# Attention front brought beside the shared projection, and six preparation operations moved from VectorE to GpSimd

## The chip, the cores and the metric

The kernel runs on one core of a Trainium2 chip. The metric is the device time of one execution in microseconds (us), lower is better; a profiled execution adds a trace of every instruction. The engines are called PE (TensorE; PEld is its weight load), DVE (VectorE), ACT (ScalarE), POOL (GpSimd) and SP (SyncE, which only issues DMAs here). Each engine works through its own queue in order.

## The reference

An input x of 4 batches, 512 tokens and 1024 features goes through four layers, each in float32. Cut to what matters:

```python
x = x + L0_attn(layernorm(x))       # attention across the batch axis
x = x + L0_ffn(layernorm(x))        # linear + top-2 of 8 LoRA experts
x = x + L1_attn(layernorm(x))       # the part that the change touches
x = x + L1_ffn(layernorm(x))        # linear + a routed mixture of LoRAs
# L1_attn:
q   = rmsnorm(x @ wq_a.T) @ wq_b.T          # 32 heads of 64 + 64 (rope)
kv  = rmsnorm((x @ wkv_a.T)[..., :64]) @ wkv_b.T
q_pe, k_pe = rope(q_pe), rope(k_pe)
p   = softmax(causal(q_full @ k_full.T * scale))
out = (p @ v) @ wo.T
```

The residual and norm lines are abridged. Per head, `wq_b` and the key part of `wkv_b` are folded into one weight, so that the scores are taken directly against the 64 normalised latent values and the 64 rotated ones; the value part of `wkv_b` is folded into the output weight.

## The kernel before, in words

A float32 product is made of three matmuls with operands split into a high and a low part (`matmul3`, L140 to L145: high by low, low by high, high by high). So each operand needs a rounding copy (the high part, mostly ACT) and a subtraction (the low part, DVE or POOL).

The stages, by the time of the profile: 0 to 76 us the batch attention, to 330 the first feed-forward layer, 330 to 425 the shared projection, 425 to about 1500 the heads, to 1580 a passage, and to the end the second feed-forward layer.

**The shared projection** (L708 to L806) goes over 16 token tiles of 128 in steps s = 0 to 16. Step s makes the product `pq` of tile s (24 matmuls of 128x384), turns tile s+2 (`turn1`: 8 transposes, with copies by ACT and DVE to `hTh`, `hTl`) and finishes tile s−1 (`keep`, L758 to L781: transposes `pn`, results `qT`, `kT` written to DRAM, per batch in `q_d`, `kT_d`, `kF_d`, `k_d`). `kf` (L744 to L755) is the key of one tile. At steps 6 and 10 weights of queries are asked for (`fetch_query`), at 8 and 12 prepared (`prepare_query`, L641 to L655, with `wql` on POOL). When the four tiles of batch 0 are done, that batch is loaded back into slot A (`load_batch`, L660: 1 MB of queries, 0.5 MB of keys); batch 1 is loaded into slot B by the heads' loop at unit 2, and every later one six units ahead.

**The heads** (loop L1171 to L1210) are 128 units u = (g, b, i): 4 groups of heads, 4 batches, 8 heads i of the group. One unit is

- `query(u)` (L678): six 128x512 matmuls of the head's weight with the batch's latent queries; `rotate_query(u)` (L690): `qf` copied by ACT (L693), two products `t` by DVE from PSUM (L695, L696), then POOL's product and sum (L697, L698); `split_query(u)` (L701): `qh` by DVE (L705) and `ql` by POOL (L706);
- `scores(u)` (L861 to L893): four query tiles, 512, 384, 256 and 128 keys wide; each is masked and copied out of PSUM by a DVE operation that also takes the row's extremum `mn` (L882), then ACT takes the exponential with `mn` as bias and adds up the row (L885). For every second unit `divisors` (L841 to L856) inverts the sums of two units on DVE, writes them to DRAM (`r_d`) and reads them back spread over partitions (`rb`), all through SP;
- `turn(u−1)` (L897): ten transposes into `pst`, three copies to `pT`, two on ACT and one on DVE;
- `context(u−3)` (L911) for every second unit: the product of values and `pT` of two units in the bank `psv`, multiplied by `rb` on DVE (L925).

**Between these** the loop advances a filler by a number of steps that `per` (L1178) gives for three places of an iteration. The filler is the output product of the batch before (`project`, L971), spread over the eight heads; in batch 0 of groups 1 to 3 it takes the first four heads, and the last four have `prepare_output` (L1015 to L1137), which makes the output weights of the group: `block` (two matmuls into the bank `poa` or `pob`), `kept` (ACT's copy to a room in SBUF), `high` (ACT), `low` and `less` (DVE, L1051 and L1055). In group 0 the preparation starts with batch 0's first head, with (0, 1, 2). Output weights come to slot C by DMA.

**What sets the order.** The program is emitted in the order of these loops, and a scheduler fixes each engine's queue from it. `tc.issue_after(ins)` holds an instruction back until behind `ins` in the order; `low` and `less` are held behind the last mask (`turn_of`), and the table load of the exponential (L804) behind the projection's last scaling (`scaled`). PSUM has eight banks: in the projection two `pt`, one `pw` (named `po`), two `pn`, three `pq`; in the heads two `pss`, two `pst`, one each of `psq`, `psv`, `poa`, `pob`.

Of the kernel before, what the change touches and what calls it, by code (L numbers as in the profile page):

```python
# [9 lines left out]
F32 = mybir.dt.float32  # L10
FR = mybir.dt.float32r
AF = mybir.ActivationFunctionType
ALU = mybir.AluOpType
# [4 lines left out]
P = 128  # L18
# [28 lines left out]
def block_kernel(ctx: ExitStack, tc: tile.TileContext, a: dict, out: bass.AP):  # L47
# [43 lines left out]
    def f32(t):  # L91
        return t.bitcast(F32)
# [564 lines left out]
    def slot(k):  # L657
        return slots[k].tile([P, ND * W1B], F32, name="slot" + "ABC"[k])
# [42 lines left out]
    def split_query(u):  # L701
# [4 lines left out]
        G.tensor_tensor(l, f[:, P:S], f32(h), ALU.subtract)  # L706
        queries[u] = f, h, l

    wqs, batches = {}, {}
    with tc.tile_pool(name="c1_w", bufs=1, side="right") as wap, \  # L710
            tc.tile_pool(name="c1_work", bufs=2) as wk, \
            tc.tile_pool(name="c1_pt", bufs=2, space=PSUM) as ptp, \
            tc.tile_pool(name="c1_pw", bufs=1, space=PSUM) as pwp, \
            tc.tile_pool(name="c1_pn", bufs=2, space=PSUM) as pnp, \
            tc.tile_pool(name="c1_pq", bufs=3, space=PSUM) as pqp:
        for ch in range(1, ND):
            split_shared(wap, ch)

# [61 lines left out]
                nc.sync.dma_start(out=kF_d[b], in_=kF)  # L780

        hts, qk, scaled = hts1, {}, [None]
        stats1[TPB - 1] = statistics([x[:, t, :] for t in order[-NB:]], "c", 4)
        for s in range(NT + 1):
            if s < NT:
                qk[s] = project(s, hts[s])
            if s + 2 < NT:
                hts[s + 2] = turn1(s + 2, ptp)
            if s > 0:
                keep(s - 1, qk[s - 1])  # L790
                if order1[s - 1] == TPB - 1:
                    batches[0, 0] = load_batch(0, 0)
            if s in (6, 10):
                wq_raw = fetch_query(s // 4 - 1)
            if s in (8, 12):
                wqs[s // 4 - 2] = prepare_query(wq_raw, pwp)
            if s in (NT - 2, NT - 1):
                query(s - NT + 2, pwp, "po")
                rotate_query(s - NT + 2)
            if s == NT - 1:  # L800
                split_query(0)

                with tc.issue_after(scaled[0].ins):
                    A.activation(first, first, AF.Exp)  # L804
# [5 lines left out]
    with ExitStack() as c2:  # L810
# [13 lines left out]
        pss = heads.enter_context(tc.tile_pool(name="c2_pss", bufs=2, space=PSUM))  # L824
        pst = heads.enter_context(tc.tile_pool(name="c2_pst", bufs=2, space=PSUM))
        psv = heads.enter_context(tc.tile_pool(name="c2_psv", bufs=1, space=PSUM))

        OF = {3: 0, 2: 512, 1: 896, 0: 1152}


        scored = [None]
        sums_of = [None]

        turn_of = [None]

        turned_in = [rdp.tile([P, 32], F32, name=f"ri{k}") for k in range(2)]
        for t in turned_in:
# [22 lines left out]

        def scores(u):  # L861

            g, b, i_ = units[u]
            f, h, l = queries.pop(u)
            _, kT, kF, _ = batches[g, b]
            p = pp.tile([P, 1280], F32, name="p")
            mn = small.tile([P, TPB], F32, name="mn")
            if i_ % 2 == 0:
                sums_of[0] = small.tile([P, 2, TPB], F32, name="rs2")
            rs2 = sums_of[0]  # L870
            rs = rs2[:, i_ % 2, :]
            for i in range(TPB - 1, -1, -1):
                n = (i + 1) * P
                ps = pss.tile([P, S], F32, name="pss")
                if i == 0:
                    scored[0] = T.matmul(ps[:, 0:n], lhsT=f[:, 0:P], rhs=kF, start=True, stop=True)
                else:
                    at = slice((i - 1) * P, i * P)
                    matmul3(ps[:, 0:n], h[:, at], l[:, at], kT[:, 0, 0:n], kT[:, 1, 0:n],
                            start=True, stop=True)  # L880
                to = p[:, OF[i] : OF[i] + n]
                turn_of[0] = V.tensor_tensor_reduce(out=to, in0=ps[:, 0:n], in1=causal[:, S - n : S], scale=1.0,  # L882
                                                    scalar=-NEG, op0=ALU.add, op1=ALU.min,
                                                    accum_out=mn[:, i : i + 1])
                A.activation(to, to, AF.Exp, bias=mn[:, i : i + 1], scale=-1.0,  # L885
                             accum_out=rs[:, i : i + 1])
                if i > 0:
                    yield
            if i_ % 2:
                divisors(u, rs2)  # L890
            probs[u] = p
            yield


# [2 lines left out]
        def turn(u):  # L897

            p = probs.pop(u)
            pTs[u] = pT = tp.tile([P, 1280], F32, name="pT")  # L900
            for copy, js in ((A.copy, (0,)), (A.copy, (3, 1)), (V.tensor_copy, (2,))):
                ps = pst.tile([P, S], F32, name="pst")
                w = 0
                for j in js:
                    for i in range(j, TPB):
                        T.transpose(ps[:, w : w + P], p[:, OF[i] + j * P : OF[i] + (j + 1) * P], ident)  # L906
                        w += P
                copy(pT[:, AT[js[0]] : AT[js[0]] + w], ps[:, 0:w])  # L908
                yield
# [105 lines left out]
        def prepare_output(g, fetched):  # L1015

            wouts[g] = {}  # L1020
            room = raw()[:, 0 : 6 * 512].rearrange("p (k n) -> p k n", k=6)
            prs = [c + k for c in range(HG // 4) for k in (0, HG // 4)]
# [24 lines left out]

            def low(kind, at):
                h, l = wouts[g][kind][-1]
                with tc.issue_after(turn_of[0].ins):  # L1050
                    V.tensor_tensor(l, src(at), f32(h), ALU.subtract)  # L1051

            def less(to, a0, a1):
                with tc.issue_after(turn_of[0].ins):
                    V.tensor_tensor(src(to), src(a0), src(a1), ALU.subtract)  # L1055

            def steps():
                block(0, 0, "a")
                yield
                kept(0, "a")  # L1060
                high("b11", "a")
                block(0, 1, "b")
                yield
                low("b11", "a")
                kept(1, "b")
                yield
                less("b", "b", 0)
                block(1, 0, "a")
                yield
                high("t1", "b")  # L1070
                kept(0, "b")
                kept(2, "a")
                high("b21", "a")
                yield
                low("t1", "b")
                low("b21", "a")
                block(1, 1, "b")
                yield
                high("b22", "b")
                kept(3, "b")  # L1080
                yield
                low("b22", "b")
                less("b", "b", 0)
                block(2, 0, "a")
                yield
                high("t2", "b")
                kept(5, "a")
                less(3, 3, 1)
                yield
                low("t2", "b")  # L1090
                less("b", 2, "b")
                high("b11", "a")
                yield
                high("t4", "b")
                high("t3", 3)
                low("b11", "a")
                yield
                low("t4", "b")
                low("t3", 3)
                block(2, 1, "a")  # L1100
                yield
                kept(1, "a")
                yield
                less("a", "a", 5)
                block(3, 0, "b")
                yield
                high("t1", "a")
                kept(5, "a")
                kept(2, "b")
                high("b21", "b")  # L1110
                yield
                low("t1", "a")
                low("b21", "b")
                block(3, 1, "a")
                yield
                high("b22", "a")
                kept(3, "a")
                yield
                low("b22", "a")
                less("a", "a", 5)  # L1120
                yield
                high("t2", "a")
                less(3, 3, 1)
                yield
                low("t2", "a")
                less("a", 2, "a")
                high("t3", 3)
                yield
                high("t4", "a")
                low("t3", 3)  # L1130
                yield
                low("t4", "a")
                yield
# [37 lines left out]
        for u in range(NU + 3):  # L1171
# [3 lines left out]
            g, b = divmod(B, NB)  # L1175
            if i == 0 and B > 0:
                filler = project(*divmod(B - 1, NB))
            per = ((4, 1, 0) if i % 2 else (1, 1, 0)) if b else (2, 2, 2) if i >= HG // 2 else (3, 3, 1)  # L1178
            if B == 0:
                per = (0, 1, 2)  # L1180
            if b == 0 and i == (HG // 2 if g else 0) and g < NG:
# [6 lines left out]
            advance(sc)  # L1188
            advance(cx)
            advance(filler, per[0])  # L1190
            if u + 1 < NU:
                split_query(u + 1)
            advance(sc)
            advance(sc)
# [3 lines left out]
            if u < NU:  # L1198
# [2 lines left out]
                    wqs[2 * g + 2] = prepare_query(wq_raw, pso, "pob")  # L1201
                if (b, i) == (0, 0) and g > 0:
                    wqs[2 * g + 1] = prepare_query(wq_raw, pso, "pob")
            if u + 2 < NU:
                query(u + 2, psq, "psq")
            if u + 2 < NU:
                rotate_query(u + 2)
            advance(filler, per[2])
            advance(tn)
# [471 lines left out]
```

## Time and profile before

| what | value |
|---|---|
| median of three runs | 1758.72 us (1757.91 to 1758.85) |
| the profiled execution | 1762.22 us, its span 1760.4 us |
| busy PE, PEld | 1714.4 us, 1433.1 us |
| busy DVE, ACT, POOL | 1311.9 us, 901.5 us, 895.7 us |
| granted clock of TensorE, mean | 0.998 of full speed |
| DMA | 228.16 MB, mean 130 GB/s |

The span runs from the first to the last recorded instruction; the rest of the profiled time lies outside it. A window row gives the length, the busy time of PE, PEld, DVE, ACT and POOL with their instruction counts, the granted clock, the share of DMA time and GB/s. A timeline row gives start, duration, engine, line, operation, output and input; in brackets stands the idle time of the engine just before it and what ended it.

### The profile page before, as it was taken

The numbers are of one execution on the slowest core, as the hardware profiler recorded it, in microseconds if no ns is written. First come the engines' busy times: TensorE is split into PE (matmuls) and PEld (weight loads), VectorE is DVE, ScalarE is ACT, GpSimd is POOL, SyncE is SP. The second block draws the span as 40 slices with busy tenths as digits, with TensorE's granted clock in tenths as the row PEclk, the third lists the DMA queues.
The fourth block names the chain that finished last, engine by engine and source line by source line (L and its number), as shares of the span: only waits on it lengthen the run. The fifth ranks groups of instructions, "written<-read, shape, count | busy, mean of one in ns | idle before, by whom it ended". The sixth has DMA issues, their size and how long they took to land.

```text
span 1760.4 us, 31605 instructions
## 1 busy us (share of the span) xinstructions
PE 1714.4 (97%) x10536; PEld 1433.1 (81%) x10536; DVE 1311.9 (75%) x3517; ACT 901.5 (51%) x2316; POOL 895.7 (51%) x902
## 2 busy tenths in 40 slices
PE   6999999999999999999999999999999999989999
PEld 6999999998677777767777767777766777789998
DVE  6977885676887777787777687777778777687675
ACT  7422331365765555575555575555466555453332
POOL 0553541203566665556566546666545665675454
PEclk9999999999999999999999999999999999999999
DMA  4313543245324234353333352343353333843431
GB/s 192 135 40 115 184 162 108 90 137 162 108 97 143 80 119 137 120 163 111 107 117 117 111 191 94 99 143 94 130 177 123 120 103 113 322 182 124 136 117 61
DMA packets 131939, 228.16 MB, mean 130 GB/s; under 512 B 22272, under 2 KB 58752, under 8 KB 128448
## 3 DMA queue, kind: packets, MB, share of 16 engines
q1 hardware_dynamic: 131776, 226.13, 39.0%
q8 instruction: 84, 1.38, 0.3%
q14 instruction: 79, 0.65, 0.1%
HBM read 156.60 MB, written 71.83 MB: 130 GB/s over the span
## 4 chain that ended last, share of the span: by engine, by line
PE 87%; DVE 6%; DMA 3%; ACT 2%; POOL 1%; issue 1%; SPq 0%; DVEq 0%; ACTq 0%; POOLq 0%
PE psv L922 9%; PE pst L906 7%; PE po L143 4%; PE po L145 4%; PE po L144 4%; PE pss L143 4%; PE pss L144 4%; PE pss L145 4%; PE poa L143 3%; PE pob L143 3%; PE psq L143 3%; PE psq L145 3%; PE psq L144 3%; PE poa L145 3%; PE poa L144 3%; PE pob L145 3%
## 5 line engine op out<-in xcount | busy, mean ns | idle before, releaser
L885 ACT ACTIVATE p<-p,mn 128x512 f32<-128x512 f32 (+3 forms) x512 | 284.4, 559 | 208.0 <-DVE mn L882 207.7
L697 POOL TENSOR_TENSOR qf<-qf,ropeT 64x512 f32<-64x512 f32 x128 | 165.5, 1293 | 274.6 <-ACT qf L693 270.5
L882 DVE CUSTOM_DVE_ANT_0 p<-pss,causal 128x512 f32<-128x512 f32 (+3 forms) x512 | 231.5, 486 | 28.4 <-PE pss L145 23.2
L698 POOL TENSOR_TENSOR qf<-qf,t 64x512 f32<-64x512 f32 x128 | 166.2, 1299 | 43.3 <-DVE t L696 35.8
L906 PE MATMUL pst<-ident,p 128*128 128x128 f32 x1280 | 186.5, 274 | 0.7 <-ACT pT L908 0.7
L906 PEld LDWEIGHTS pst<-ident,p 128*128 128x128 f32 x1280 | 153.8, 141 | 26.0 <-ACT pT L908 2.7
L908 ACT COPY pT<-pst 128x512 f32<-128x512 f32 x256 | 141.7, 580 | 44.8 <-PE pst L906 43.7
L706 POOL TENSOR_TENSOR ql<-qf,qh 128x384 fp32r<-128x384 f32 x128 | 129.9, 1015 | 62.1 <-DVE qh L705 62.1
L143 PE MATMUL pss<-kT,ql 128*128 128x512 f32 (+2 forms) x384 | 144.6, 376 | 4.0 <-POOL ql L706 1.5
L957 POOL TENSOR_TENSOR cxl<-s,cxh 128x256 fp32r<-128x256 f32 x128 | 97.4, 768 | 88.5 <-ACT cxh L956 60.7
L143 PE MATMUL po<-w_h,hTl 128*128 128x384 f32 (+1 forms) x384 | 133.1, 347 | 1.1 <-DVE x L398 1.1
L144 PE MATMUL pss<-kT,qh 128*128 128x512 f32 (+2 forms) x384 | 130.9, 341 | 0.0
L145 PE MATMUL pss<-kT,qh 128*128 128x512 f32 (+2 forms) x384 | 130.3, 339 | 0.0
L145 PE MATMUL po<-w_h,hTh 128*128 128x384 f32 (+1 forms) x384 | 130.1, 339 | 0.0
L144 PE MATMUL po<-w_l,hTh 128*128 128x384 f32 (+1 forms) x384 | 129.7, 338 | 0.0
L908 DVE COPY pT<-pst 128x256 f32<-128x256 f32 x128 | 54.1, 423 | 94.1 <-PE pst L906 93.3
L693 ACT COPY qf<-psq 128x512 f32<-128x512 f32 x126 | 73.8, 586 | 67.7 <-PE psq L145 67.1
L695 DVE TENSOR_TENSOR t<-psq,ropeT 32x512 f32<-32x512 f32 x126 | 87.7, 696 | 23.4 <-ACT qf L693 19.4
L143 PEld LDWEIGHTS pss<-kT,ql 128*128 128x128 f32 x384 | 72.7, 189 | 35.4 <-POOL ql L706 11.4
L885 ACT ACTIVATION_READ_ACCUMULATOR p<-p,mn 128x1 f32 x512 | 97.3, 190 | 0.0
L696 DVE TENSOR_TENSOR t<-psq,ropeT 32x512 f32<-32x512 f32 x126 | 87.1, 691 | 1.8
L999 DVE TENSOR_TENSOR xs<-xs,pob 128x512 f32<-128x512 f32 x105 | 71.2, 678 | 19.4 <-PE pob L145 19.2
(564 smaller groups left out, 4961.1 us busy)
## 6 DMA issues: line engine op xcount, KB each, us to landing
xs<-x_d SPq DMA_DIRECT2D x128, 256.0 KB
x_d<-xs SPq DMA_DIRECT2D x128, 256.0 KB
slotC<-in_woT_dram SPq DMA_DIRECT2D x32, 512.0 KB
rb<-r_d SPq DMA_DIRECT2D x128, 128.0 KB
w_t<-raw SPq DMA_DIRECT2D x32, 288.0 KB
x<-in_x_dram SPq DMA_DIRECT2D x16, 512.0 KB
x_d<-x SPq DMA_DIRECT2D x32, 256.0 KB
slotA<-q_d SPq DMA_DIRECT2D x8, 1024.0 KB
```

What stands on the lines that cost most here:

```text
L143: T.matmul(ps, lhsT=al, rhs=bh, start=start, stop=False, **kw)
L144: T.matmul(ps, lhsT=ah, rhs=bl, start=False, stop=False, **kw)
L145: T.matmul(ps, lhsT=ah, rhs=bh, start=False, stop=stop, **kw)
L697: G.tensor_tensor(f[mid], f[mid], ropeT[mid, 0, :], ALU.mult)
L698: G.tensor_tensor(f[mid], f[mid], t2[mid], ALU.add)
L706: G.tensor_tensor(l, f[:, P:S], f32(h), ALU.subtract)
L882: turn_of[0] = V.tensor_tensor_reduce(out=to, in0=ps[:, 0:n], in1=causal[:, S - n : S], scale=1.0, scalar=-NEG, op0=ALU.add, op1=ALU.min, ...
L885: A.activation(to, to, AF.Exp, bias=mn[:, i : i + 1], scale=-1.0, accum_out=rs[:, i : i + 1])
L906: T.transpose(ps[:, w : w + P], p[:, OF[i] + j * P : OF[i] + (j + 1) * P], ident)
L908: copy(pT[:, AT[js[0]] : AT[js[0]] + w], ps[:, 0:w])
L922: T.matmul(ps[n * KVR : (n + 1) * KVR, S - w : S], lhsT=k[:, j, :], rhs=pTs[u + n][:, AT[j] : AT[j] + w], start=(j == 0), stop=(j == TPB - 1))
L957: G.tensor_tensor(l, src, f32(h), ALU.subtract)
```

## The change: what it does

1. The queries of units 0 to 3 are made in steps 9, 10, 13 and 15 of the shared projection (before: units 0 and 1 in steps 14 and 15, 2 and 3 in the heads' loop). Units 0, 1 and 2 are split one step after.
2. The masked scores of units 0 and 1 (`AHEAD = 2`) are made in steps 11 to 14, two tiles a step, through one PSUM bank of their own; `pq` has two banks instead of three. They go to the room of slot B and a spare `kT` tile, so that batch 1's loads have to wait until both units are turned. Their exponentials are issued behind the projection's last scaling, and the divisors of unit 1 behind unit 3's second mask.
3. In `prepare_output`, `low` and `less` go to POOL where no operand is in PSUM: twice each `low("b22", 3)`, `less(3, 3, 1)` and `low("t3", 3)`, six operations in each of the four groups. `b22`'s low part is now made from the copy in SBUF instead of from PSUM, with `high` still from PSUM.
4. In batch 0 of groups 1 to 3, `per` is (3, 2, 2) instead of (2, 2, 2) for heads 4 and 5.

```diff
+    def masked_scores(u, psp, p):
+        g, b, _ = units[u]
+        f, h, l = queries.pop(u)
+        _, kT, kF, _ = batches[g, b]
+        mn = small.tile([P, TPB], F32, name="mn")
+        masked[u] = p, mn
+        for i in range(TPB - 1, -1, -1):
...
+            turn_of[0] = V.tensor_tensor_reduce(out=p[i], in0=ps[:, 0:n],
...
+    AHEAD = 2
...
+            tc.tile_pool(name="c1_ps", bufs=1, space=PSUM) as psp1, \
...
-            tc.tile_pool(name="c1_pq", bufs=3, space=PSUM) as pqp:
+            tc.tile_pool(name="c1_pq", bufs=2, space=PSUM) as pqp:
...
+        at_step = {9: 0, 10: 1, 13: 2, 15: 3}
+        spare = slot(1), inp.tile([P, 2 * S], F32, name="kT")
...
-            if s in (NT - 2, NT - 1):
-                query(s - NT + 2, pwp, "po")
-                rotate_query(s - NT + 2)
+            if s == 9:
+                ahead = [masked_scores(u, psp1, by_tile(spare[0], spare[1] if u else None))
+                         for u in range(AHEAD)]
+            if s in (11, 12, 13, 14):
+                for _ in range(2):
+                    next(ahead[(s - 11) // 2])
+            if s in (9, 10, 13, 15):
+                query(at_step[s], pwp, "po")
+                rotate_query(at_step[s])
+            if s - 1 in (9, 10, 13):
+                split_query(at_step[s - 1])
             if s == NT - 1:
-                split_query(0)
...
+                with tc.issue_after(scaled[0].ins) if u < AHEAD else ExitStack():
+                    A.activation(p[i], p[i], AF.Exp, bias=mn[:, i : i + 1], scale=-1.0,
+                                 accum_out=rs[:, i : i + 1])
+                if i == TPB - 2 and u == AHEAD + 1:
+                    with tc.issue_after(turn_of[0].ins):
+                        divisors(AHEAD - 1, sums_ahead[-1])
...
             def low(kind, at):
                 h, l = wouts[g][kind][-1]
+                if at not in po:
+                    G.tensor_tensor(l, src(at), f32(h), ALU.subtract)
+                    return
...
             def less(to, a0, a1):
+                if not {to, a0, a1} & set(po):
+                    G.tensor_tensor(src(to), src(a0), src(a1), ALU.subtract)
+                    return
...
-                low("b22", "b")
+                low("b22", 3)
...
-                low("b22", "a")
+                low("b22", 3)
...
-            per = ((4, 1, 0) if i % 2 else (1, 1, 0)) if b else (2, 2, 2) if i >= HG // 2 else (3, 3, 1)
+            per = ((4, 1, 0) if i % 2 else (1, 1, 0)) if b else (2 + (i < HG // 2 + 2), 2, 2) if i >= HG // 2 else (3, 3, 1)
...
-            if u + 1 < NU:
+            if AHEAD < u + 1 < NU:
                 split_query(u + 1)
...
-            if u + 2 < NU:
+            if AHEAD + 2 <= u + 2 < NU:
                 query(u + 2, psq, "psq")
-            if u + 2 < NU:
                 rotate_query(u + 2)
```

More of the change, by code (lines that the diff above doesn't have):

```diff
@@ L707, in split_query, with by_tile @@
         queries[u] = f, h, l
+    turn_of, scored, masked = [None], [None], {}
+    OF = {3: 0, 2: 512, 1: 896, 0: 1152}
+    def masked_scores(u, psp, p):
[5 more added lines that the diff above has]
+        for i in range(TPB - 1, -1, -1):
+            n = (i + 1) * P
+            ps = psp.tile([P, S], F32, name="pss")
+            if i == 0:
+                scored[0] = T.matmul(ps[:, 0:n], lhsT=f[:, 0:P], rhs=kF, start=True, stop=True)
+            else:
+                at = slice((i - 1) * P, i * P)
+                matmul3(ps[:, 0:n], h[:, at], l[:, at], kT[:, 0, 0:n], kT[:, 1, 0:n],
+                        start=True, stop=True)
+            turn_of[0] = V.tensor_tensor_reduce(out=p[i], in0=ps[:, 0:n],
+                                                in1=causal[:, S - n : S], scale=1.0,
+                                                scalar=-NEG, op0=ALU.add, op1=ALU.min,
+                                                accum_out=mn[:, i : i + 1])
+            yield
+    def by_tile(room, other=None):
+        if other is None:
+            return {i: room[:, OF[i] : OF[i] + (i + 1) * P] for i in OF}
+        at = 1280
+        to = {1: other[:, 0 : 2 * P]}
+        for i in (3, 2, 0):
+            to[i] = room[:, at : at + (i + 1) * P]
+            at += (i + 1) * P
+        return to
+    AHEAD = 2
     wqs, batches = {}, {}
@@ L826, in block_kernel @@
         psv = heads.enter_context(tc.tile_pool(name="c2_psv", bufs=1, space=PSUM))
[L828 to L834, printed above, removed]
+        sums_of, sums_ahead = [None], []
         turned_in = [rdp.tile([P, 32], F32, name=f"ri{k}") for k in range(2)]
@@ L861, in scores @@
         def scores(u):
[L863 to L867, printed above, removed]
+            i_ = units[u][2]
+            part = masked_scores(u, pss, by_tile(pp.tile([P, 1280], F32, name="p"))) if u >= AHEAD else None
             if i_ % 2 == 0:
@@ L870, in scores @@
             rs2 = sums_of[0]
+            if u < AHEAD:
+                sums_ahead.append(rs2)
             rs = rs2[:, i_ % 2, :]
             for i in range(TPB - 1, -1, -1):
[L873 to L886, printed above, removed]
+                if part is not None:
+                    next(part)
+                p, mn = masked[u]
+                with tc.issue_after(scaled[0].ins) if u < AHEAD else ExitStack():
[4 more added lines that the diff above has]
+                        divisors(AHEAD - 1, sums_ahead[-1])
                 if i > 0:
                     yield
-            if i_ % 2:
+            if i_ % 2 and u >= AHEAD:
                 divisors(u, rs2)
-            probs[u] = p
+            probs[u] = masked.pop(u)[0]
             yield
@@ L905, in turn @@
                     for i in range(j, TPB):
-                        T.transpose(ps[:, w : w + P], p[:, OF[i] + j * P : OF[i] + (j + 1) * P], ident)
+                        T.transpose(ps[:, w : w + P], p[i][:, j * P : (j + 1) * P], ident)
                         w += P
```

## The prediction

> **What bounds the kernel now.** I read the page first: busy shares, then the chain of waits, then the table of windows by stage, then TensorE's own list of waits and its timeline where the list points. PE is busy 1714.4 of 1760.4 us, so the sum of everything a change can win by filling PE is 46 us, and most of that lies outside the stages touched.
>
> ```profile
> PE 1714.4 (97%) x10536; PEld 1433.1 (81%) x10536; DVE 1311.9 (75%) x3517; ACT 901.5 (51%) x2316; POOL 895.7 (51%) x902
> ...
> PE 87%; DVE 6%; DMA 3%; ACT 2%; POOL 1%; issue 1%; SPq 0%; DVEq 0%; ACTq 0%; POOLq 0%
> ```
>
> By windows (length, then busy us of PE, PEld, DVE, ACT, POOL, granted clock, DMA): the shared projection is 330 to 425, the start of the heads 425 to 500, the bulk of the heads 500 to 1500.
>
> ```profile
> 330.00:425.00 95.00, 91.97 (x581) 88.89 (x579) 68.64 (x254) 55.80 (x186) 12.04 (x18) 1.00 0.47 142
> 425.00:500.00 75.00, 72.50 (x381) 50.21 (x382) 58.54 (x163) 53.16 (x141) 39.08 (x34) 0.95 0.43 131
> 500.00:1500.00 1000.00, 992.11 (x5488) 755.99 (x5488) 749.52 (x1991) 574.71 (x1585) 580.57 (x568) 1.00 0.38 122
> ```
>
> The reader is to see two small holes: the clock of 0.95 in the second row, and 7.9 us idle in the third. PE's waits (us in total, times, longest) and its timeline name them.
>
> ```profile
> PE poa L143 <- DVE t41l L1051: 3.2, 3, 1.1
> ...
> PE pn L766 <- DVE kf L755: 1.7, 3, 0.8
> ...
> PE pss L143 <- POOL ql L706: 1.5, 5, 0.7
> PE pss L143 <- DVE mn L882: 1.3, 2, 1.2
> ```
>
> ```profile
> 424.97 0.47 PE L143 MATMUL pss<-kT,ql 128*128 128x512 f32 x1 [0.48 <-DVE t L696]
> 427.57 0.58 PE L143 MATMUL pss<-kT,ql 128*128 128x256 f32 x1 [1.16 <-DVE mn L882]
> 429.19 0.76 PE L143 MATMUL pss<-kT,ql 128*128 128x512 f32 x1 [0.16 <-DVE mn L882]
> 436.76 0.50 PE L143 MATMUL pss<-kT,ql 128*128 128x512 f32 x1 [0.66 <-POOL ql L706]
> 441.75 0.50 PE L143 MATMUL pss<-kT,ql 128*128 128x512 f32 x1 [0.32 <-POOL ql L706]
> ```
>
> ```profile
> 428.00:429.00 1.00, 1.00 (x5) 0.74 (x4) 0.57 (x4) 1.00 (x4) 0.00 (x0) 0.50 0.93 311
> ```
>
> So where the heads start, PE has nothing but scores to do and each step waits for DVE or POOL: .48+1.16+.16+.66+.32 = 2.8 us idle. In that slice the granted clock is 0.50, and it stays so from about 427.5 to 434.3. I add up the slowed matmuls (a 128x512 group of three took 1.42 us instead of 0.69, a 384 group 0.96 instead of 0.52, and so on): about 3.2 us. Together **6.0 us** are lost here.
>
> **Part 1, the front of the heads.** Queries 0 and 1 were already made in the shared projection, at steps 14 and 15; now 0 to 3 are made at 9, 10, 13, 15, and the scores of units 0 and 1 at 11 to 14. PE does the same work: a query is six matmuls, 1.47 us from the first to what follows it; the four score tiles of a unit about 1.9 us. Two queries and two units moved are 2×1.47+2×1.9 = 6.7 us, put into a stage in which PE is already full. Moving earns nothing; only holes do.
> What goes: the 6.0 us above, and one stall in the projection of 0.76 us. There PE waits at 391.9 for kf, which DVE makes late; query 0 now stands in front of that transpose, 1.47 us of cover: −0.8. (The first query wants batch 0's queries from a DMA issued at 380.5 and landed by 387.2 at the latest by the queue's order, wanted at 386.4: 0 to 0.8, taken as 0.)
> What comes, in the projection: DVE runs in order. A split (the cast qh) waits for POOL's second rotation, and behind it stand hTl of the next tiles, kf, and the new masks:
>
> ```profile
> 420.38 0.36 DVE L705 CAST qh<-qf 128x384 fp32r<-128x384 f32 x1 [1.46 <-POOL qf L698]
> ```
>
> The scores there have one PSUM bank, so tile 2 of unit 0 cannot begin before DVE has masked tile 3. Placing the new DVE work (t 0.70 twice, qh 0.36, masks 0.68 and 0.55) by hand among the old rows of steps 10 to 14, I find one place where PE arrives first: DVE reaches the first mask at about 404.2 and PE wants the bank 1 us before; with the mask that is +1.65. Bounds: 0 if the cast is not late, 5.0 if all three splits do it.
> What comes, after the projection: the last kf still leads the last transposes, so that wait (0.55) stays. Then PE goes to unit 2's scores; DVE's split of query 3 waits for POOL as in the row above (1.0 to 1.5): +1.45. Against that, PE has the scores of two units behind it and the transposes of unit 0 near, but these need the exponentials of units 0 and 1, which the change holds back until after the projection's last scaling and the table load (1.28 us). ACT then has about 2.3 us of exponentials per unit, three units, before the order is as before: bounds 0 to 0.8 for PE; I take 0, since two blocks of preparation (1.0 us each) and unit 3's scores stand in between.
> Sum of part 1: −6.0 −0.8 +1.65 +1.45 = **−3.7**, if the clock holds. Whether it does cannot be read from the trace: the drop followed 424.1 to 427.5, of which PE streamed only about 1.6 us. After the change that stretch has about as much or a little more. If it falls again, up to 3.2 come back.
> [...]
>
> **Loads.** Batch 1's queries and keys go into slot B, which holds the spare scores; their DMAs were issued at 418.7 and 420.3 and now wait for the transposes of unit 1, about 441. SP issues in order, and the divisors' rb of units 0 and 1 stands behind them: 1.5 MB at the 4.5 us that a load behind as much took (asked at 385.96, landed 390.45) makes rb land at about 447.5, after its own short way. DVE wants rb at about 450, PE wants slot B from 457 on. Hidden by 2 to 3 us; with that cover gone, DVE's queue stops at the product with rb and every mask behind it.
>
> **Part 2, six operations on POOL.** Per group two each of b22's low part, one difference and t3's low part leave DVE; POOL gets 6×1.3 = 7.8 us (by the ql, wql and L698 rows: 1343 ns for cxl's neighbour al, 1299 for L698), DVE loses about 2×0.69+0.69+1.68+2×0.68 = 5.1. The 1.68 is one row:
>
> ```profile
> 780.40 1.68 DVE L1051 TENSOR_TENSOR t31l<-raw,t31h 128x512 fp32r<-128x512 f32 x1
> 782.33 0.68 DVE L1051 TENSOR_TENSOR t41l<-poa,t41h 128x512 fp32r<-128x512 f32 x1
> 783.07 0.50 PE L143 MATMUL poa<-b110h,cxl 128*128 128x512 f32 x1 [1.06 <-DVE t41l L1051]
> ```
>
> t31l has both operands in SBUF and took 1.68 us where its twin with a PSUM operand took 0.68; POOL's L697 ran at 780.24 to 781.52, just that long. t41l stood behind it, and PE's bank poa behind t41l: 1.06 us, in each of three groups. With t31l on POOL, and t41l one preparation step earlier for two units (per 3 instead of 2), all of it goes: **−3.2**.
> Against it, POOL is in order too, and ql, without which no scores start, now stands behind these operations. Groups 1 to 3: POOL has holes of 3.7 and 4.3 us in the two places (idle before L697 at 757.2 and 780.2). b22's low part and the difference fit; the third operation ends about 781.4 to 782.6, then L697, cxl and ql follow: ql was already 0.18 late there. Bounds 0 to 1.7 at the first place, 0 to 0.7 at the second; I take 0.35 a group together, +1.0. Group 0 has no such holes: between the rotation of unit 7 and its ql stand now 1.3+0.75+1.3+1.3 us of POOL work, ACT's copy for t3 among it. By hand ql is ready at 468.1 where PE wants it at 465.3, 2.8; the second place gives 0.5 to 1.8. Bounds 0 to 4.6. I take +1.5, nearer to the waits for ql that the trace shows (0.18 to 0.66) than to the hand count, because preparation blocks and transposes can stand in front of the late scores.
>
> [...]
>
> **Sum.** −3.7 +1.5 −3.2 +1.0 = −4.4 against the profiled execution: 1762.2 − 4.4 = 1757.8 (span 1760.4 and 1.8 outside it). That execution lies 3.5 above the median of the runs shown, 1758.7, so: **1754.3**, −0.25%. About 0.2%, 3.5 us, is what a measurement of this kernel can tell from no change.
>
> **Rivals.**
> *The clock falls again, or ACT is late.* For it: PE's stretch after the projection is as thin as before and ACT starts with a table load. Against: two blocks and a score unit more are ready. It gives back 3.2 (or 0.8): 1755 to 1758, no difference that can be told.
> *ql late behind POOL's new work (slower).* At every group's two places and in group 0 the upper bounds hold: 4.6+3×2.4 = 11.8 instead of the 2.5 I counted. With the −3.7 and −3.2 kept that is +4.9: 1763.6. It decides from a lateness of 6.9 in all (no gain) and shows as slower from 10.4. For it: POOL's order and the group 0 count. Against: the holes of 4 us.
> *All of it works.* No new wait in the projection, no late ql: −6.8−3.2−0.5 (small waits of DVE) = −10.5: 1748.
> *It does not do what it says:* rb or slot B late, so that what PE wins by 440 it waits for by 457; then only the groups' −2.2 +1.5 remain: 1758.
>
> **Numbers.** Forecast (1751 to 1757) 0.42, all works 0.13, clock or ACT 0.18, late loads 0.07, slower 0.20. The range reaches from the best case to the slow one: 1748 to 1764. Faster by over 0.2% means below 1755.2: three quarters of the forecast, the best case and some of the clock case, 0.50; within 0.28; slower (above 1762.2) 0.22.
>
> **What would show it.** Right: clock 1.00 in every window of the transition; the wait of poa for t41l gone; POOL's busy time up by about 31 us, DVE's down by about 20; a wait of pss for mn in the projection of about 1.7. Wrong: pss for ql above 4 us in PE's list; cx waiting for rb; clock 0.50 again at 430; a wait of po for slot A at the first query.

## The result: slower by 0.23%

The changed kernel takes 1762.98 us (median of 22 runs, 1757.09 to 1767.43) against 1758.79 us before (22 runs, 1757.32 to 1761.59): a ratio of 1.0023, 95% interval 1.0017 to 1.0029. The forecast was 1754.3. The sign is wrong: +4.2 us where −4.4 was forecast.

The profile after, first the lines that answer to those of before. The page's busy times and chain:

```profile
PE 1716.0 (97%) x10536; PEld 1434.9 (81%) x10536; DVE 1300.4 (74%) x3493; ACT 903.1 (51%) x2316; POOL 923.1 (52%) x926
...
PE 85%; DVE 6%; POOL 4%; DMA 2%; ACT 2%; issue 1%; SPq 0%; POOLq 0%; DVEq 0%; ACTq 0%
```

POOL has 24 instructions and 27.4 us more, and 4% of the chain instead of 1%. DVE lost 11.5 us, not the 20 that I had reckoned, although the 24 operations took 19.4 us on it before. The windows of the three stages:

```profile
330.00:425.00 95.00, 91.88 (x571) 89.19 (x572) 69.09 (x245) 50.53 (x169) 17.33 (x19) 0.98 0.39 118
425.00:500.00 75.00, 68.28 (x359) 44.80 (x357) 49.89 (x154) 52.48 (x146) 37.67 (x34) 1.00 0.47 146
500.00:1500.00 1000.00, 996.06 (x5521) 760.84 (x5523) 747.02 (x1984) 581.52 (x1597) 603.53 (x590) 1.00 0.38 123
```

The bulk of the heads has become denser (996.1 busy where it was 992.1). The start of the heads has become emptier (68.3 busy where it was 72.5). PE's waits, and the places of the largest in its timeline:

```profile
PE pss L143 <- POOL ql L706: 5.7, 6, 2.8
PE pss L143 <- DVE mn L731: 3.0, 2, 2.1
...
PE pn L808 <- DVE kf L797: 1.0, 2, 0.6
```

```profile
405.25 0.69 PE L143 MATMUL pss<-kT,ql 128*128 128x384 f32 x1 [2.12 <-DVE mn L731]
434.22 0.47 PE L143 MATMUL pss<-kT,ql 128*128 128x512 f32 x1 [0.48 <-DVE t L696]
436.57 0.39 PE L143 MATMUL pss<-kT,ql 128*128 128x256 f32 x1 [0.89 <-DVE mn L731]
474.89 0.50 PE L143 MATMUL pss<-kT,ql 128*128 128x512 f32 x1 [2.83 <-POOL ql L706]
500.55 0.64 PE L143 MATMUL pss<-kT,ql 128*128 128x512 f32 x1 [1.79 <-POOL ql L706]
```

The 3.2 us for t41l are gone from the list. In their place stand 2.1 us at the first mask in the projection and 4.6 us for ql in group 0. In this profile the half clock no longer stands at the start of the heads. It follows the gaps at 405 and 500, as one microsecond of each place shows (the granted clock is the third number from the right, 0.50):

```profile
406.00:407.00 1.00, 1.00 (x4) 1.00 (x4) 0.69 (x3) 0.00 (x0) 0.00 (x0) 0.50 1.03 419
501.00:502.00 1.00, 1.00 (x4) 0.81 (x3) 0.97 (x4) 0.89 (x2) 0.45 (x1) 0.50 0.53 213
```

Each of these two falls lasted 3.41 us (405.17 to 408.58 and 500.75 to 504.16); the one in the profile that I predicted from lasted 6.83 us (427.48 to 434.31). A gap alone does not bring it, though: behind the longest one here, the 2.83 us before 474.89, the clock stays at 1.00.

Two measures are used below. **The clock's loss** of a run is (1 − its mean granted clock) times its span, if PE is busy throughout. The clock is recorded to three decimals, so one run's loss is known to 0.9 us. It averages 1.6 to 2.4 us in the sets of runs of the kernel before and 5.2 us in the 22 of the changed one. **The stretch** is the time in a profile from the shared projection's first product to the start of the multiplication of the sixth context product by rb, which is at 517.6 in the second profile of the kernel before. It holds the same 1061 matmuls in all kernels. **The passage** is the place in it where the heads start, from about 424 to 435 us in the kernel before.

### The profile page after: what moved, and what is told of

Same layout as the page of the kernel before. It is cut to its first block, busy times and chain, and to the rows that moved or that the text cites. A ratio compares the mean times of both kernels' runs of the same rounds, so it can differ in the third digit from the quotient of the medians.

```text
span 1761.2 us, 31620 instructions
## 1 busy us (share of the span) xinstructions
PE 1716.0 (97%) x10536; PEld 1434.9 (81%) x10536; DVE 1300.4 (74%) x3493; ACT 903.1 (51%) x2316; POOL 923.1 (52%) x926
## 4 chain that ended last, share of the span: by engine, by line
PE 85%; DVE 6%; POOL 4%; DMA 2%; ACT 2%; issue 1%; SPq 0%; POOLq 0%; DVEq 0%; ACTq 0%
PE psv L961 8%; PE pst L945 7%; PE po L143 4%; PE po L145 4%; PE po L144 4%; PE pss L143 4%; PE pss L144 4%; PE pss L145 3%; PE pob L143 3%; PE poa L143 3%; PE psq L143 3%; PE psq L145 3%; PE psq L144 3%; PE pob L145 3%; PE pob L144 3%; PE poa L145 3%
## 5 line engine op out<-in xcount | busy, mean ns | idle before, releaser
L921 ACT ACTIVATE p<-p,mn 128x512 f32<-128x512 f32 x504 | 280.4, 559 | 206.5 <-DVE mn L731 206.0
L731 DVE CUSTOM_DVE_ANT_0 p<-pss,causal 128x512 f32<-128x512 f32 x504 | 229.6, 486 | 23.1 <-PE pss L145 18.7
```

Source lines behind the costliest of these rows:

```text
L731: turn_of[0] = V.tensor_tensor_reduce(out=p[i], in0=ps[:, 0:n], in1=causal[:, S - n : S], scale=1.0, scalar=-NEG, op0=ALU.add, op1=ALU.min ...
L921: A.activation(p[i], p[i], AF.Exp, bias=mn[:, i : i + 1], scale=-1.0, accum_out=rs[:, i : i + 1])
```

## The experiments

All medians stand beside 1758.8 to 1759.4 us for the kernel before, run with them. Stretch and half clock are those of one profile each; the first profile of the kernel before, the one that I predicted from, has 188.3 and 6.8.

| kernel | median us | ratio, 95% interval | stretch us | at half clock in it, us |
|---|---|---|---|---|
| before, second profile | 1758.59 | 1.0002 [0.9993, 1.0010] | 185.4 | 0 |
| changed | 1762.98 | 1.0023 [1.0017, 1.0029] | 196.1 | 6.8 |
| front alone | 1767.21 | 1.0052 [1.0040, 1.0065] | 194.5 | 3.4 |
| POOL's part alone | 1753.44 | 0.9972 [0.9960, 0.9984] | 187.4 | 3.4 |
| POOL's part in groups 1 to 3 | 1752.35 | 0.9963 [0.9950, 0.9975] | 185.9 | 3.4 |
| changed, group 0 on DVE | 1760.38 | 1.0008 [1.0000, 1.0017] | 195.0 | 6.8 |
| changed, late split | 1761.01 | 1.0009 [1.0000, 1.0018] | 192.4 | 3.4 |
| front, pairs held at the start | 1764.93 | 1.0041 [1.0028, 1.0055] | 191.5 | 3.4 |
| the same, and late split | 1762.84 | 1.0027 [1.0018, 1.0036] | 188.8 | 0 |
| front, pairs held everywhere | 1763.14 | 1.0019 [1.0010, 1.0028] | 192.7 | 10.2 |
| before, pairs held everywhere | 1753.77 | 0.9968 [0.9957, 0.9979] | 183.2 | 0 |
| POOL's part, pairs held | 1754.18 | 0.9969 [0.9959, 0.9978] | 188.4 | 6.8 |
| extra steps alone | 1761.71 | 1.0008 [1.0000, 1.0017] | 186.8 | 6.8 |
| POOL in groups 1 to 3, no extra steps | 1756.55 | 0.9986 [0.9977, 0.9995] | 185.7 | 3.4 |
| changed, all mended | 1753.15 | 0.9969 [0.9957, 0.9981] | 188.3 | 0 |
| POOL in groups 1 to 3, pairs held | 1749.20 | 0.9942 [0.9930, 0.9954] | 183.8 | 3.4 |

### The kernel before, profiled again

No edit.

> The kernel before, unchanged, to see how its profile differs from one execution to the next. Theory A (the execution that I predicted from was an outlier: it had two TensorE windows of 3.4 us at half clock, which most executions do not have, so that the 3.2 us I counted as a gain were already missing from the median): the profile here shows no or one such window, a mean clock of 0.999 or 1.000, and a time of 1758 to 1760 us. Rival: the thin stretch at 428 always brings the clock down; clock 0.998 again and a profiled time near 1762.

What this expectation and two later ones call a window of TensorE is a stretch of 3.41 us, the shorter of the two lengths that a fall had here; the 6.83 us of the first profile make two, and half of one is 1.7 us. For this profile theory A holds (mean clock 0.999; 1760.63 us, just above its range). The passage ran at full clock, and the stretch took 185.4 us where the profile that I predicted from has 188.3: 2.9 us less without the 6.8 us at half clock.

```profile
420.00:430.00 10.00, 7.70 (x36) 5.32 (x34) 7.54 (x30) 7.51 (x24) 4.74 (x7) 1.00 0.89 296
430.00:440.00 10.00, 8.44 (x49) 6.93 (x49) 7.53 (x24) 7.17 (x22) 7.12 (x6) 1.00 0.28 89
```

It is not that PE had more to do there. These are the 3.4 us ahead of the fall in the first profile, and the same place in the second, which has no fall behind it:

```profile
424.10:427.50 3.40, 1.77 (x7) 1.17 (x7) 2.25 (x7) 1.41 (x5) 2.06 (x2) 1.00 0.95 287
423.54:426.94 3.40, 1.80 (x7) 1.18 (x7) 2.26 (x8) 1.42 (x5) 2.05 (x2) 1.00 0.85 273
```

But the fall is no accident of one execution, as theory A had it. Nine profiles here are of kernels with the front not moved, and seven of them have half clock in the passage, from 424.2 to 427.5 on, for 3.41 us (four) or 6.83 us (three). If a matmul takes twice as long there, that is 1.9 us on average over the nine. This is an estimate: in the profile after, the starts of 128x384 matmuls lie 0.32 us apart at half clock (406.37 to 407.97) and 0.17 to 0.18 at full clock (411.59 to 411.94), which would give 1.7. Of the eight profiles with the front moved, four have it at the new start of the heads, from 433.7 to 436.9 on, on average over the eight 1.3 us; falls elsewhere in the stretch add 0.9. One microsecond from each kind, POOL's part in groups 1 to 3 and the front alone:

```profile
427.00:428.00 1.00, 1.00 (x5) 0.88 (x4) 0.70 (x2) 0.59 (x4) 0.27 (x1) 0.50 0.88 244
437.00:438.00 1.00, 1.00 (x5) 0.94 (x5) 0.67 (x4) 1.00 (x5) 0.28 (x1) 0.50 0.04 12
```

### The two parts, each alone

Front alone: part 2 of the change (items 3 and 4 of its list) undone. POOL's part alone: the kernel before with

```diff
+                if at not in po:
+                    G.tensor_tensor(l, src(at), f32(h), ALU.subtract)
+                    return
...
+                if not {to, a0, a1} & set(po):
+                    G.tensor_tensor(src(to), src(a0), src(a1), ALU.subtract)
+                    return
...
-                low("b22", "b")
+                low("b22", 3)
...
-            per = ((4, 1, 0) if i % 2 else (1, 1, 0)) if b else (2, 2, 2) if i >= HG // 2 else (3, 3, 1)
+            per = ((4, 1, 0) if i % 2 else (1, 1, 0)) if b else (2 + (i < HG // 2 + 2), 2, 2) if i >= HG // 2 else (3, 3, 1)
```

> The changed kernel with the six operations a group back on DVE and the old number of preparation steps, so only the heads' front is moved. Theory A (the front costs: PE waits 2.1 us for the first mask at step 11, its clock falls there, and the idle time that it removes was small): 1761 to 1764 us, 2 to 5 us slower than before, with the wait of pss for mn at about 405 in PE's list. Rival B (the front is neutral or a gain, all of the loss is POOL's in group 0): 1756 to 1759.

> The kernel before with the six operations a group on POOL and the extra preparation steps, so the front is not moved. Theory A: group 0 loses the 4.6 us that PE waits for ql, groups 1 to 3 gain about 2.5 each by the profiles' lag: 1755 to 1758. Rival B (all of the loss is here): 1761 to 1764.

Both theories were too small: the front costs 8.4 us, POOL's part gains 5.4. I had them at −3.7 and −0.7. The sum of the parts, +3.0, is near the measured +4.2.

The front's 9.1 us in the stretch (194.5 − 185.4) hold the mask's wait of 2.13 and about 1.7 of slow clock (at the passage; none follows the mask's gap in this profile), and little other idle time. So starts tell more here than idle times. The context product and a block are made of matmuls 64 columns wide, and where the halves of a pair stand next to each other in PE's order, four records took 1.08 us; two of one half took 1.07. In the second profile of the kernel before (a row's second number is its busy time, the last its count):

```profile
440.71 2.37 PE L922 MATMUL psv<-pT,slotA 128*64 128x512 f32 x16
...
444.65 1.08 PE L1031 MATMUL poa<-slotC 128*64 128x512 f32 x4
```

In the front alone:

```profile
442.73 1.07 PE L1071 MATMUL poa<-slotC 128*64 128x512 f32 x2
443.74 0.44 PE L945 MATMUL pst<-ident,slotB 128*128 128x128 f32 x2
444.11 1.07 PE L961 MATMUL psv<-pT,slotA 128*64 128x512 f32 x2
```

So in these rows two of them ran side by side where they stood together. The half that was ready first was put into a gap of the schedule, and the other half came later, alone. PE counts as busy in both cases, so no list of waits shows it. The time in 64-column matmuls (from each start to PE's next one, counted up to 1.05 ns for each of the 128 to 512 values in a row of the output, half of the 1.07 us by 512, so that waits stay out) is 24.1 us in the stretch before, 28.0 with the front alone, 26.0 with the change. In the rest of the heads it is 159.3 before and with the front alone, 156.3 with POOL's part: the pairs had been broken there too, and POOL's part mends some of them.

### Group 0 back on DVE

```diff
-                if at not in po:
+                if g and at not in po:
...
-                if not {to, a0, a1} & set(po):
+                if g and not {to, a0, a1} & set(po):
...
-                low("b22", 3)
+                low("b22", 3 if g else "b")
...
-                low("b22", 3)
+                low("b22", 3 if g else "a")
```

> The changed kernel with group 0's six operations back on DVE, the other groups' on POOL. Both theories: the waits of pss for ql of 2.8 and 1.8 us in group 0 go, and with them the half clock behind them: 4 to 6.5 us less than the changed kernel, 1756.5 to 1759. If the time does not fall, the waits for ql were only where another wait shows first (group 0 limited by DVE).

The waits for ql go as expected, but only 2.6 us of time with them, less than either theory gave: the time in 64-column matmuls rises by 2.0 us (28.0 for 26.0). That the queue was the cause is read from POOL's timeline in the changed kernel:

```profile
467.10 1.29 POOL L698 TENSOR_TENSOR qf<-qf,t 64x512 f32<-64x512 f32 x1 [0.16 <-DVE t L696]
468.47 1.29 POOL L1091 TENSOR_TENSOR b220l<-raw,b220h 128x512 fp32r<-128x512 f32 x1
469.71 0.95 POOL L996 TENSOR_TENSOR cxl<-cx,cxh 128x256 fp32r<-128x256 f32 x1
470.62 1.27 POOL L1098 TENSOR_TENSOR raw<-raw 128x512 f32<-128x512 f32 x1
472.62 1.26 POOL L1091 TENSOR_TENSOR t30l<-raw,t30h 128x512 fp32r<-128x512 f32 x1 [0.73 <-ACT t30h L1085]
473.85 0.99 POOL L706 TENSOR_TENSOR ql<-qf,qh 128x384 fp32r<-128x384 f32 x1
```

Between unit 7's rotation and its ql stand three moved operations and ACT's copy for the third. It is the count of the prediction, 2.83 where that had 2.8.

### POOL's part in groups 1 to 3, and its two halves

POOL in groups 1 to 3: the edit of POOL's part, with the condition `g and`. Extra steps alone: the line of `per`. No extra steps: all but that line.

> The kernel before with the six operations on POOL and the extra steps in groups 1 to 3 alone; group 0 stays as it was. Theory: by the milestones of the run with POOL in all groups, groups 1 to 3 gave -1.6, -2.8 and -2.3 us and group 0 nothing (its waits for ql of 2.3 us were made up by better pairing of half-width matmuls): 1752 to 1753.5, the same as with all groups. Rival (group 0 on POOL costs its ql waits): 1750 to 1751.5.

> The kernel before with the extra preparation steps for heads 4 and 5 in groups 1 to 3 alone; no operation moves to POOL. Theory (the gain in groups 1 to 3 comes from DVE being freed of t31l, whose 1.68 us stood before t41l): about nothing, 1757.5 to 1759.5, and the three waits of poa for t41l stay. Rival (the order does it: t41l is asked for earlier): 2 to 4 us less and the waits gone.

> The kernel before with the six operations on POOL in groups 1 to 3, and the old number of preparation steps. Theory: the larger part of the gain of both together (7.1 us): 1752 to 1755, the waits of poa for t41l under 1 us in all, and 2 to 3 us less time in 64-column matmuls. Rival (POOL's order holds ql back without the extra steps): 1757 to 1759 with waits of pss for ql above 2 us.

The first theory holds: groups 1 to 3 alone give 1752.35, at least as good as all groups. The halves fit neither theory fully. The extra steps alone take t41l's wait away too, against my theory. But three others come or grow (1.1, none and 0.7 us in the second profile of the kernel before), and the time is not lower (1761.71, 2.7 above the kernel before; its clock's loss is 2 us larger). The waits in its list:

```profile
PE pss L143 <- DVE mn L882: 2.9, 3, 1.6
PE psv L922 <- DVE cx L925: 2.5, 2, 1.8
PE pst L906 <- ACT pT L908: 2.0, 3, 0.7
```

POOL's operations without the extra steps gain 2.5 us. The wait for ql rises to 2.8 us (1.5 before), and the one for DVE's sums of the output product is larger (0.9 before):

```profile
PE pob L143 <- DVE xs L999: 4.3, 4, 1.2
```

Together they gain 7.1. So the gain needs both: DVE freed of the six operations, and the steps drawn forward into the room that this leaves.

### Unit 1's split behind the masks

```diff
-                split_query(at_step[s - 1])
+                with tc.issue_after(turn_of[0].ins) if s == 11 else ExitStack(): split_query(at_step[s - 1])
```

> The changed kernel with one edit: at step 11 the split of unit 1's query stands behind the two masks of unit 0 in DVE's order. Theory (DVE stood 1.5 us in the split's wait for POOL with the first mask behind it, PE lost 2.1 us, and the thin stretch brought half a TensorE window of clock): the wait of pss for mn at 405 falls under 0.6, no clock drop there, 2 to 3.8 us less: 1759 to 1761. Rival (the mask would be late anyway, h and hTl stand in front of it): less than 1 us.

The theory holds: 2.0 us less (at the edge of its range), the wait is 0.31 where it was 2.12, and no half clock follows it. DVE's order in the changed kernel shows the queue, the cast that stands for POOL and the mask behind it:

```profile
401.62 0.36 DVE L705 CAST qh<-qf 128x384 fp32r<-128x384 f32 x1 [1.47 <-POOL qf L698]
401.89 0.81 DVE L134 TENSOR_SCALAR h<-x,mvc,rstdc 128x1024 f32<-128x1024 f32 x1
...
404.50 0.68 DVE L731 CUSTOM_DVE_ANT_0 slotB<-pss,causal 128x512 f32<-128x512 f32 x1
```

With the late split:

```profile
402.35 0.44 PE L143 MATMUL pss<-kT,ql 128*128 128x384 f32 x1 [0.31 <-DVE mn L731]
```

### Half-width pairs held together

The later unit's half first, and the other issued behind it, for every context product (in one run for group 0's first batch alone):

```diff
-                for n in range(2):
-                    T.matmul(ps[n * KVR : (n + 1) * KVR, S - w : S], lhsT=k[:, j, :],
+                for n in (1, 0):
+                  with ExitStack() if n else tc.issue_after(mm.ins):
+                    mm = T.matmul(ps[n * KVR : (n + 1) * KVR, S - w : S], lhsT=k[:, j, :],
...
```

On the front alone, on POOL's part, on POOL's part in groups 1 to 3, and on the kernel before:

> The front alone (POOL's part undone), with the two half-width matmuls of each context product held together: the later unit's half first, the other behind it. Theory (in the front alone 4 us of the loss are half-width matmuls that run singly where a pair would share the time): psv pairs start 0.01 us apart, the time in 64-column matmuls to the sixth context product falls from 28.0 to 24 or 25 us, 2.5 to 4 us less than the front alone: 1763 to 1764.7. Rival (PE waits for ACT's exponentials and copies there anyway, and single halves only fill the gaps): under 1 us less, 1766.5 to 1767.5, with idle time of PE in its place.

> POOL's part alone (front not moved), with the half-width matmuls of each context product held together. Theory: few pairs are still broken there, about four in each group of which each costs 0.2 to 0.5 us: 1 to 3 us less than POOL's part alone, 1750.5 to 1752.5, the fastest so far. Rival: the held half makes PE wait elsewhere, no gain: 1753 to 1755.

> POOL's part in groups 1 to 3, front not moved, with the half-width matmuls held together. Theory: 1 to 2 us below the same without holding, 1750 to 1752, the fastest. Rival (as in the run with POOL in all groups, holding gives no gain, since what PE saves it waits for elsewhere): 1752 to 1754.

> The kernel before with the half-width matmuls of every context product held together, nothing else: the control for the same edit on the front alone. If holding pairs gains here too, that share of the 4.1 us which it gained on the front alone is no cost of the front. Theory: the passage has whole pairs already, groups 1 to 3 gain 0 to 1 us each: 1756 to 1758.8. Rival (holding is worth 4 us on any kernel): 1754 to 1755.5.

Held everywhere it gains 4.1 us on the front, in the range of the theory, and 5.0 on the kernel before, against my theory: the edit is worth its time on a kernel without the front. So the 4.1 are not all a cost of the front, and the run that holds pairs at the start alone was needed. On POOL's part in all groups it gives nothing (1754.18 for 1753.44; neither interval excludes the other), on groups 1 to 3 another 3.2. Why it gives nothing with group 0 on POOL is not settled; the 64-column time fell there as well (21.2 for 22.1 in the stretch, 153.0 for 156.3 after it). POOL's part in groups 1 to 3 with pairs held is the fastest kernel here, 1749.20, 9.8 us under the kernel before.

> The front alone (POOL's part undone), with the half-width matmuls held together in the first batch of group 0 only, so groups 1 to 3 run as in the front alone. Theory (single halves at the start are 4 us of the front's cost): 1763 to 1764.5. Rival (the gain of holding them everywhere came from groups 1 to 3): 1766 to 1767.5.

> As the run before, and unit 1's split behind unit 0's masks. Theory: the mask's 2 us and half a clock window go as well: 1760.5 to 1762.5, and what is left above the kernel before, 2 to 3 us, is the front's own (a passage as thin as before, with other waits added). Rival (the two stalls are all of the front's cost): 1758 to 1759.5.

Held at the start alone, the front takes 1764.93, 2.3 us less (a little above the range of the theory). With the late split as well it takes 1762.84, 2.1 less again. So the front's 8.4 us are 2.3 by the halves, 2.1 by the mask and **4.0 that remain** (the theory had 2 to 3). The 8.4, the 4.0 and the 4.4 of both edits together are clear of the spread of the runs; the 2.3 and the second 2.1 taken singly are not (1765.95 to 1770.54 in the runs of the front alone, 1763.67 to 1769.87 and 1760.40 to 1769.07 in the others). The late split's 2.0 on the changed kernel is. In the profiles the time in 64-column matmuls falls by 3.6 us (28.0 to 24.4), but a wait of 1.46 us for ql comes that the front alone does not have. What remains is read from the last of these, whose profile has no slow clock in the stretch; PE's waits there:

```profile
430.17 0.47 PE L143 MATMUL pss<-kT,ql 128*128 128x512 f32 x1 [0.48 <-DVE t L696]
432.51 0.39 PE L143 MATMUL pss<-kT,ql 128*128 128x256 f32 x1 [0.89 <-DVE mn L731]
436.74 0.49 PE L726 MATMUL pss<-kF,qf 128*128 128x128 f32 x2 [0.30 <-DVE mn L731]
...
477.38 0.50 PE L143 MATMUL pss<-kT,ql 128*128 128x512 f32 x1 [1.46 <-POOL ql L706]
...
499.91 0.47 PE L143 MATMUL pss<-kT,ql 128*128 128x512 f32 x1 [0.40 <-DVE mn L731]
```

The passage is still there: units 2 and 3 now stand where 0 and 1 stood, with nothing behind them. Adding up by hand how much each start lies beyond its usual distance, where that is over 0.24 us, the passage loses about 3.5 us instead of 5.2, a gain of 1.7. The mask in the projection still costs 0.9, and the units up to the sixth context product lose some 3.4 in waits for ACT's copies, ql and masks that the second profile of the kernel before does not have. The stretch is 3.4 us longer; 2.6 of it are in these sums, 0.8 are not placed. The 1.46 us for ql came with the held pairs, so part of the 4.0 is the price of that edit and not of the front.

### The changed kernel, mended

Late split, group 0 on DVE, pairs held everywhere.

> The changed kernel with three edits: unit 1's split behind unit 0's masks, group 0's six operations back on DVE, and the half-width matmuls of a context product held together. Theory (the front itself is worth nothing once its own stalls are gone, as the clock's loss in the kernel before is 2 us on average and the idle 2.8 us come back in another form): 1751 to 1755, no better than POOL's part in groups 1 to 3 alone at 1752.4. Rival (the front hides the passage when its stalls are gone, as the change intends): 1746 to 1750.

1753.15: the theory holds. The same without the front takes 1749.20, so the front costs 4.0 us here as well. Of this, 1.8 us of the stretch are still time in 64-column matmuls (23.0 with the front, 21.2 without): the edit holds the context products' pairs only, and the blocks' (poa and pob) take 8.9 us with the front and 7.6 without.

## Why the prediction was wrong, by its steps

**The passage, −6.0: this step failed.** 3.2 of it were the half clock of the one execution that the profile shows. At this place a kernel with the front not moved loses 1.9 us on average over nine profiles, and moving the front does not win that: the eight profiles with it lose 1.3 at the new place and 0.9 at others in the stretch. Also, that execution had lost 3.4 us to the clock where the runs of the kernel before lose 1.6 to 2.4 on average, so part of the 3.2 was missing from the median already, and I subtracted the whole 3.5 us between execution and median once more at the end. The other 2.8 were idle time, of which moving two units away takes 1.7 at best, and the run with both stalls mended shows it given back by 500 us.

**The sentence "PE does the same work. Moving earns nothing": failed.** It put the price of the new order at nothing. The same matmuls take longer in another order: 3.9 us more in 64-column matmuls in the profile (28.0 for 24.1), 2.3 us by the run with pairs held at the start.

**The stall at the first mask, +1.65: right,** 2.12 in the profile and 2.0 to 2.1 by two pairs of runs. **The split after the projection, +1.45: right in kind:** .48, .89 and .30 are there, in all 1.7.

**kf, −0.8:** no wait is left at the place, as said; the second profile of before has about 0.4 there, so the term was at most half as large. **Loads, 0: right.** Neither PE nor DVE waits for slot B or rb.

**Group 0's ql, +1.5: mis-sized by choice.** The hand count of 2.8 and up to 1.8 was what came, 2.83 and 1.79, and the sign of being wrong that I had named, more than 4 us for ql in PE's list, with it (5.7). I took a third of it because blocks and transposes could stand in front; they did not. Yet undoing it gains only 2.6, for the reason above, so in time the term was nearer than the waits say.

**Groups 1 to 3, −3.2 + 1.0: right in sign, too small.** t41l's wait went from the list, ql's hardly rose, and the gain is 7.1 by the run with POOL there alone. 3.0 us of 64-column time (159.3 to 156.3) account for much of what I did not see; the parts are not additive, as the halves show.

**DVE beside POOL:** the sum has no term for DVE slowed by POOL's new work. In the profile after, DVE's products, sums and differences beside the 24 moved operations took 0.68 to 0.70 us, each with one operand in PSUM. But DVE's 128 sums of 128x256 (L948, after L987), which read two operands from SBUF, took 66.6 us in all before and 71.4 after: 0.37 to 0.42 each with POOL idle, and up to 1.20 before and 1.19 after beside POOL's rotations and ql, whose places shifted. These 4.8 us are part of why DVE won less than the 20 us; that PE waited for them is not shown.

**The clock:** I held that it might fall again at the passage. In the profile after it fell at two of the new stalls instead; in four of the seven others with the front moved it fell at the passage. How busy PE is does not tell it: with 1.8 busy us of 3.4 the first profile of the kernel before has the fall behind them, and the second, with the same 1.8, keeps 1.00. Taking the clock's loss off each run, the medians are 1757.8 for the changed kernel and about 1757.0 before: three quarters of the 4.2 us go with the clock, if PE would have been busy in all of those windows. That is worked out, not measured by an experiment. By the same working the front alone costs about 7.9 us and POOL's part gains about 6.0, so in the parts the clock is the smaller share.

**The slower rival** had 1763.6, close to the measured 1763.0 by luck: it had ql late in group 0 and at every group's places. In group 0 it came true, 4.6 as priced. In groups 1 to 3 it did not, and POOL's part as a whole gains. What makes the kernel slower is the front, which I had as the larger gain.

## What to carry to other kernels

Before a slow clock in a profile is counted as a gain, profile the same kernel again, and ask whether the change takes the thin place away or only moves it: here seven of nine profiles had half clock in the passage before, and four of eight at its new place after. Moving the first work of a stage into a full one before it moves the gap to the next work in line, so ask what then has nothing behind it. And where matmuls run in pairs, compare starts between neighbours: PE is listed as busy with a lone half for as long as with two (1.07 and 1.08 us here).

## What the runs showed of the hardware

Granted clock: each fall to half inside the span lasted 3.41 or 6.83 us, and the two profiles of the kernel before have it at different times (427.5 and 1549.1 us). Over 22 runs of the changed kernel the mean clock went from 0.994 to 1.000, and the time with it, 1767.0 at 0.994 and 1757.1 at 1.000. A gap of PE of 2.12 us at 403 to 405 and one of 1.79 at 499 to 501 came before falls in the profile of the changed kernel. The length of the gap does not decide it: 2.83 us in the same profile and 2.13 us in the front alone had none behind them. What decides is open.

Half-width matmuls: two 128x512 matmul records of one 64-column half took 1.07 us, four of both halves 1.08 us.
